# Seven rounds of weight pieces behind the softmaxes, maxima two ahead, and two late stores behind loads, in a graph network with cross-attention

## The chip, the core and the metric

The kernel runs on one core of a Trainium2 chip. The metric is the device time of one launch in microseconds (us). In the profile PE is the matrix engine (TensorE), DVE the vector engine (VectorE), ACT the scalar engine (ScalarE), POOL is GpSimd, and SP (SyncE) issues nearly all DMAs. Each engine works through its own queue in order; an instruction that has to wait holds all that stand behind it on that engine. This holds for SP's queue of DMA issues too.

## The reference

A graph network over 1024 nodes with 512 features: normalise, one graph convolution, four layers of cross-attention and a gated feed-forward network (FFN), one more graph convolution. Cut to its core:

```
def _attn(xf, cond, Wq, Wk, Wv, Wo):          # 16 batches of 64 nodes, 256 condition rows each, 8 heads of 64
    q = (xb @ Wq); k = (cond @ Wk); v = (cond @ Wv)
    att = einsum('bnhd,bmhd->bhnm', q, k) * DH ** (-0.5)
    w = softmax(att, axis=-1)
    o = einsum('bhnm,bmhd->bnhd', w, v)
    return (o @ Wo)

h = _gcn(batchnorm(x))
for i in range(4):
    h = h + _attn(_ln(h), cond, Wq[i], Wk[i], Wv[i], Wo[i])
    u = _ln(h) @ geglu_w[i] + geglu_b[i]       # 512 x 4096
    val, gate = split(u, 2)
    h = h + (val * gelu(gate)) @ ffo_w[i] + ffo_b[i]
h = _gcn(h)
return h + x_in
```

## The kernel before

**Parts.** Matrix products are made from split operands. A matrix is cut into a high part, a low part and a third one (high less low), and three products are summed. So every operand passes through ACT (high part), DVE (low part) and DVE or GpSimd (third part) before PE reads it. For the condition these are `ah_c`, `al_c`, `as_c` (GpSimd's subtraction makes `as_c`, L301); in layer 0 they are made on the way and stored, and in layers 1 to 3 they are loaded as `ch`, `cl`, `cs`.

**Attention.** The 16 batches form eight groups g of two batches (128 nodes). The loop over g = 0 to 5 makes, in each iteration, the keys k of group g+1, its first values v, the mix (`po`, L845) of group g, the scores `sc` of group g+1 (L811), the remaining values, and the output projection (`oy`, `ox`, L883 and L888) of group g, whose operands are `oh` (ACT, L869), `ol` and `os` (DVE, L872 and L873). The last group's softmax stands outside the loop; what is called g=6 below is the work around it, where DVE follows program order. "The softmax of group 5" is traced in iteration g=4.

**Softmax.** `scores` (L800) handles four banks u. For each: DVE takes the maximum `nmax_u` (L818), ACT two exponentials with sums (L823), DVE the reciprocal (L826) and two multiplies (L828) on `pr`. Then PE turns `pr` around (`tr_pr`).

**Weight pieces.** The FFN's up-projection computes a part of its columns from weight blocks that are split into parts ahead of time, during the attention loop. `stage` (L912) splits one 128 x 256 piece: ACT the high part (L917), DVE the low (L918) and third part (L919), then a store into `half_dram` (plain pieces, 8 of them) or `chunk_dram` (14 pieces, of two chunks with seven each, some of them sums and differences made by DVE at L950 to L963). The pieces rotate through two buffers, `gs2`; a piece can only be begun when the store of the piece before the last has landed. `staged` (L922) is a generator that is advanced by eight steps at the end of iterations 3, 4 and 5. Its loads (`gp`, `gx`) are issued in the step that first needs them.

**Order.** PE's order is written out (`pin`). For the other engines a scheduler picks the order from the dependencies and the program order; `in_order`, `issue_after` and `waiting_for` add such dependencies. So a piece of code that is traced elsewhere shifts what stands ahead of what on ACT, DVE and SP.

**Start of the FFN.** Two stages of columns are multiplied first (`g`, L994); DVE writes the gated result `fT` (L1016) and SP stores it to `f_dram` (`Gated.store`, L1233), from which the down-projection reads it much later. Then come chunks: the first two are read from `chunk_dram` (`ga`, `gb`, L1202 and L1214, used at L1109), the others are loaded as raw weights (`gxa`, `gxb`, L1071), summed by GpSimd (L1081) and split by ACT and DVE (`gha`, L1047, L1048). ACT scales PE's results (L1123) and applies the gates (L1138).

Of the kernel before, what the change touches and what calls it, by code (L numbers as in the profile page):

```python
# [9 lines left out]
F32 = mybir.dt.float32  # L10
# [5 lines left out]
OP = mybir.AluOpType  # L16
AX = mybir.AxisListType

P = 128
# [7 lines left out]
def gnn_kernel(  # L27
# [26 lines left out]
    nc = tc.nc  # L54
# [41 lines left out]
    @contextmanager  # L96
    def in_order(engine):

        traced = nc.cur_bb.bb.instructions
        n = len(traced)  # L100
        before = next((i for i in reversed(traced) if i.engine == engine), None)
        yield
        for i in traced[n:]:
            if i.engine == engine:
                if before is not None:
                    tc.add_manual_dep(i, before.name, mybir.DependencyInfo(
                        mybir.DependencyClass.NoSync, mybir.DependencyReason.DATA))
                before = i

    def bank(name):  # L110
        return psum.tile([P, 512], F32, tag="bank", name=name)
# [673 lines left out]
    def acc_tile(name):  # L785
        return accs.tile([P, 512], F32, tag="acc", name=name)
# [13 lines left out]
    def scores(l, g, qT, kT):  # L800


        c0 = (g % 4) * P
        probs = {}
        banks = [bank(f"sc_{l}_{g}_{u}") for u in range(4)]
        for c2 in range(2):
            for a in range(2):
                for j in range(2):
                    pj = slice(j * DH, (j + 1) * DH)
                    for b in range(2):  # L810
                        pin(nc.tensor.matmul(  # L811
                            banks[2 * c2 + j][b * NPG:(b + 1) * NPG, a * M:(a + 1) * M],
                            qT[g // 4][c2][pj, a, c0 + b * NPG:c0 + (b + 1) * NPG],
                            kT[c2][pj, a, b * M:(b + 1) * M], start=True, stop=True))
        for u in range(4):
            ps3 = banks[u].rearrange("p (a m) -> p a m", a=2)
            nmax = small.tile([P, 2], F32, tag="nmax", name=f"nmax_{l}_{g}_{u}")
            nc.vector.tensor_reduce(nmax, ps3, AX.X, OP.max, negate=True)  # L818
            pr = t512(f"pr_{l}_{g}_{u}")
            pr3 = pr.rearrange("p (a m) -> p a m", a=2)  # L820
            tot = small.tile([P, 2], F32, tag="tot", name=f"tot_{l}_{g}_{u}")
            for a in range(2):
                nc.scalar.activation(pr3[:, a, :], ps3[:, a, :], AF.Exp,  # L823
                                     bias=nmax[:, a:a + 1], accum_out=tot[:, a:a + 1])
# [88 lines left out]
    def stage(x, to, name):  # L913

        t = three_halves(f"gs2_{name}")
        h, low, third = (t[:, i * M:(i + 1) * M] for i in range(3))
        nc.scalar.mul(twelve_bits(h), x, INWARD * TINY)  # L917
        nc.vector.scalar_tensor_tensor(twelve_bits(low), h, -1.0 / TINY, x, OP.mult, OP.add)  # L918
        nc.vector.tensor_tensor(twelve_bits(third), h, low, OP.subtract)  # L919
        nc.sync.dma_start(to, t.rearrange("p (w f) -> p w f", w=3))  # L920

    def staged(l):  # L922

        for j in range(2):
            for n in range(2):
                x = acc_tile(f"gp_{l}_{j}_{n}")
                of = geglu_w[l][2 * n * P:2 * (n + 1) * P, j * DFF:j * DFF + PLAIN * P]
                nc.sync.dma_start(x.rearrange("p (k f) -> p k f", k=2),
                                  of.rearrange("(k p) f -> p k f", p=P))
                for k in range(2):  # L930
                    yield
                    stage(x[:, k * M:(k + 1) * M], half_dram[j, 2 * n + k], f"{l}_{j}_{n}_{k}")
        for c in range(PLAIN, KC):
            name = f"{l}_{c}"
            pairs = []
            for k in range(2):
                t = acc_tile(f"gx_{name}_{k}")
                for j in range(2):
                    of = geglu_w[l][2 * k * P:2 * (k + 1) * P, j * DFF + c * P:j * DFF + (c + 1) * P]
                    nc.sync.dma_start(columns_of(t)[:, j], of.rearrange("(k p) f -> p k f", p=P))  # L940
                pairs += [t[:, :M], t[:, M:]]
            a11, a21, a12, a22 = pairs
            s1, s2 = (rows.tile([P, M], F32, tag="gy", name=f"gy{i}_{name}", bufs=2)
                      for i in range(2))

            def put(x, i):
                stage(x, chunk_dram[c - PLAIN, SPLIT.index(i)], f"{name}_{i}")

            yield
            nc.vector.tensor_tensor(s1, a21, a22, OP.add)  # L950
            put(a22, 3)
            yield
            nc.vector.tensor_tensor(s2, s1, a11, OP.subtract)
            put(s1, 4)
            yield
# [4 lines left out]
            yield  # L960
            put(a12, 1)
            yield
            nc.vector.tensor_tensor(a12, a12, s2, OP.subtract)  # L963
            put(s2, 5)
            yield
            put(a12, 2)
            yield

    class HalfWeights:

# [85 lines left out]
    def columns_of(t):  # L1056
        return t.rearrange("p (b k c) -> p b k c", k=2, c=P)

    class Chunk:


        def __init__(self, l, r, c):
            self.n, self.c = f"{l}_{r}_{c}", c
            self.cv = l * 2 * DFF // P + r * KC + c
            self.x = [flat(slot(f"gxa_{self.n}")), t512(f"gxb_{self.n}")]
            self.x.append(rows.tile([P, M], F32, tag="gy", name=f"gy_{self.n}", bufs=2))
            for k, n in enumerate((2, 1)):
                for j in range(2):
                    c0 = j * DFF + r * D + c * P
                    of = geglu_w[l][2 * k * P:2 * (k + 1) * P, c0:c0 + P]  # L1070
                    nc.sync.dma_start(columns_of(self.x[k])[:, n * j],  # L1071
                                      of.rearrange("(k p) f -> p k f", p=P))
            self.parts = [None, None, None]

        def sums(self):
# [385 lines left out]
    for l in range(L):  # L1461
# [166 lines left out]
        for g in range(NG - 2):  # L1628
# [56 lines left out]
        for _ in staging:  # L1685
            pass
        g = NG - 2
        last = l == L - 1
        f_first = Gated(l, 0)
# [398 lines left out]
```

## Time and profile before

| | |
|---|---|
| median of 3 runs | 2278.33 us (2275.65 to 2283.69) |
| profiled execution | 2280.34 us |
| its span in the profile | 2278.4 us |
| granted PE clock | 0.998 of full speed |
| DVE busy | 1722.1 us |
| ACT busy | 1155.4 us |
| GpSimd busy | 507.4 us |

The profile describes one execution. A timeline row gives the start, the duration, the engine, the line and operation, "output <- input", how many like instructions are put together (x4), and in brackets the idle time ahead of it and what ended that. Rows of waits give the engine and its instruction, what it waited for, and then total us, times, longest us. `[0.77 <-DMA ga<-chunk_dram]` reads: idle for 0.77 us, until the load of `ga` from `chunk_dram` had landed. SPq rows are DMA issues, whose duration is that of the issue and not of the transfer.

### The profile page before, as it was taken

What the parts mean: (1) busy time and instruction counts of PE and PEld (TensorE: products, weight loads), DVE (VectorE), ACT (ScalarE), POOL (GpSimd) and SP (SyncE); (2) the same over time, 40 slices, a digit from 0 to 9 for tenths busy, and PEclk for the clock granted to TensorE, in tenths of its full rate; (3) what the DMA queues carried; (4) which work ended last, traced back from release to release, by engine and by line L of the source; (5) the groups of instructions that cost most, each with busy time, mean ns of one, the idle gap of its engine ahead of it and who ended that gap; (6) DMA issues with size and microseconds to landing.
All of it is one profiled execution on the core that took longest, in us unless ns stands there. A gap on an engine that the chain in (4) does not pass through costs nothing. (4 is left out here: it accounts for less than half of the span.)

```text
span 2278.4 us, 35747 instructions
## 1 busy us (share of the span) xinstructions
PE 2241.9 (98%) x12768; PEld 1807.5 (79%) x12768; DVE 1722.1 (76%) x3296; ACT 1155.4 (51%) x2313; POOL 507.4 (22%) x487
## 2 busy tenths in 40 slices
PE   8999999999999999999999999999999999999999
PEld 5678778788888878788888888878888887878787
DVE  9886676999965466899976466889976465789965
ACT  7555546565345445565346445555426445556521
POOL 1121201387000000177000000178100000058301
PEclk9999999999999999999999999999999999999999
DMA  5154554433425264443533364353543355353551
GB/s 171 57 185 167 209 208 140 138 120 130 167 111 194 80 243 172 130 128 102 194 129 142 118 228 174 96 169 102 179 163 135 125 176 197 107 169 111 179 184 54
DMA packets 216952, 340.83 MB, mean 150 GB/s; under 512 B 16488, under 2 KB 117168, under 8 KB 216768
## 3 DMA queue, kind: packets, MB, share of 16 engines
q1 hardware_dynamic: 214672, 333.05, 42.8%
q0 software_dynamic: 1376, 4.30, 0.6%
q8 instruction: 105, 1.72, 0.3%
q10 hardware_dynamic: 720, 1.11, 0.1%
q14 instruction: 79, 0.65, 0.1%
HBM read 236.69 MB, written 101.72 MB: 149 GB/s over the span
## 5 line engine op out<-in xcount | busy, mean ns | idle before, releaser
L1123 ACT ACTIVATE g<-g 128x512 f32<-128x512 f32 x224 | 131.3, 586 | 190.4 <-PE g L1109 187.6
L1581 POOL TENSOR_TENSOR ln3T<-ln3T,ln3T 128x512 f32<-128x512 f32 x8 | 13.3, 1659 | 885.5 <-DVE ln3S L1574 885.5
L1288 PE MATMUL fx<-bs_wff,as_f 128*128 128x512 f32 x512 | 158.8, 390 | 0.0
L1288 PE MATMUL fy<-bl_wff,al_f 128*128 128x512 f32 x512 | 158.6, 390 | 0.0
L1288 PE MATMUL fy<-bh_wff,ah_f 128*128 128x512 f32 x512 | 157.7, 389 | 0.0
L292 ACT ACTIVATE ah_f<-fr 128x1024 fp32r<-128x1024 f32 x64 | 67.9, 1060 | 173.6 <-DVE al_f L293 80.2
L823 ACT ACTIVATE pr<-sc,nmax 128x256 f32<-128x256 f32 x256 | 118.3, 472 | 58.6 <-DVE nmax L818 58.6
L818 DVE TENSOR_REDUCE nmax<-sc 128x2 f32<-128x512 f32 x128 | 84.1, 679 | 77.5 <-PE sc L811 77.5
L361 ACT ACTIVATE k<-k 128x512 f32<-128x512 f32 x125 | 72.8, 585 | 116.5 <-PE k L350 116.5
L361 ACT ACTIVATE v<-v 128x512 f32<-128x512 f32 x127 | 74.5, 587 | 100.5 <-PE v L350 100.4
L1053 POOL TENSOR_TENSOR gsa<-gha,gla 128x512 fp32r<-128x512 f32 x96 | 122.6, 1301 | 6.1 <-DVE gla L1048 6.1
L1109 PE MATMUL g<-gr,gha 128*128 128x512 f32 x384 | 118.2, 389 | 0.0
L1288 PEld LDWEIGHTS fy<-bl_wff,al_f 128*128 128x128 f32 x512 | 96.1, 188 | 21.5 <-DVE bl_wff L1265 1.6
L1288 PEld LDWEIGHTS fx<-bs_wff,as_f 128*128 128x128 f32 x512 | 96.1, 188 | 21.4 <-DVE bs_wff L1269 1.7
L1288 PEld LDWEIGHTS fy<-bh_wff,ah_f 128*128 128x128 f32 x512 | 96.1, 188 | 20.0
L350 PE MATMUL v<-bh_wv,ch 128*128 128x512 f32 x384 | 106.9, 400 | 1.2 <-ACT pr L823 1.2
L293 DVE SCALAR_TENSOR_TENSOR al_f<-ah_f,fr 128x1024 fp32r<-128x1024 f32 x64 | 78.1, 1220 | 35.6 <-ACT ah_f L292 29.5
L350 PE MATMUL k<-ch,bh_wk 128*128 128x512 f32 x384 | 104.0, 392 | 0.0
L350 PE MATMUL v<-bl_wv,cl 128*128 128x512 f32 x384 | 103.1, 390 | 0.0
L350 PE MATMUL v<-bs_wv,cs 128*128 128x512 f32 x384 | 103.0, 391 | 0.0
L350 PE MATMUL k<-cl,bl_wk 128*128 128x512 f32 x384 | 102.8, 389 | 0.0
L350 PE MATMUL k<-cs,bs_wk 128*128 128x512 f32 x384 | 101.6, 395 | 0.6 <-ACT k L361 0.6
(333 smaller groups left out, 5956.8 us busy)
## 6 DMA issues: line engine op xcount, KB each, us to landing
f_dram<-fT SPq DMA_DIRECT2D x128, 256.0 KB, 2.0
fr<-f_dram SPq DMA_DIRECT2D x64, 512.0 KB, 4.6
ch<-cond_dram SPq DMA_DIRECT2D x48, 512.0 KB, 4.9
cl<-cond_dram SPq DMA_DIRECT2D x48, 512.0 KB, 6.5
cs<-cond_dram SPq DMA_DIRECT2D x48, 512.0 KB, 7.8
chunk_dram<-gs SPq DMA_DIRECT2D x56, 384.0 KB, 2.4
wff<-in_L_gnn_ffo_w_dram SPq DMA_DIRECT2D x32, 512.0 KB, 5.4
half_dram<-gs SPq DMA_DIRECT2D x32, 384.0 KB, 3.5
```

What stands on the lines that cost most here:

```text
L292: nc.scalar.mul(twelve_bits(h), x, INWARD * TINY)
L293: left_parts.low = nc.vector.scalar_tensor_tensor(twelve_bits(l), h, -1.0 / TINY, x, OP.mult, OP.add)
L350: pin(nc.tensor.matmul(self.bank, twelve_bits(left[k // 2])[:, k % 2, self.c * P:(self.c + 1) * P], twelve_bits(right[k // 2])[:, k % 2, : ...
L361: nc.scalar.mul(self.bank, self.bank, 1.0 + TINY)
L818: nc.vector.tensor_reduce(nmax, ps3, AX.X, OP.max, negate=True)
L823: nc.scalar.activation(pr3[:, a, :], ps3[:, a, :], AF.Exp, bias=nmax[:, a:a + 1], accum_out=tot[:, a:a + 1])
L1053: split_left.last = pin(t.tensor_tensor(s_at, h_at, l_at, OP.subtract))
L1109: pin(nc.tensor.matmul(to, self.part(i, which)[:, k, :], self.rights[i][which].bitcast(F32R)[:, k, :], start=start and k == 0, stop=stop a ...
L1123: pin(nc.scalar.mul(to, to, 1.0 + TINY))
L1288: pin(nc.tensor.matmul(to, twelve_bits(left[which][0])[:, k, b * P:(b + 1) * P], twelve_bits(right[which])[:, k, :], start=u == 0 and whic ...
L1581: t.tensor_tensor(b12, b22, b12, OP.subtract)
```

## The change

Three edits.

*Softmax.* Two maxima are traced ahead of the loop over u, and each turn of it takes the maximum of u + 2 behind its reciprocal.

*Pieces.* `staged` becomes seven rounds, each of which splits three or four pieces. A round's loads are issued a round ahead (`fetch`), and its instructions are put behind everything that DVE and ACT have been given so far (`behind_traced`). The rounds stand: in the iteration of g=3 in the key loop (i == 1), behind the softmax, and at the end; in that of g=4 in the key loop and behind the softmax; in that of g=5 in the key loop; the first loads are issued in that of g=2. The three places of "eight steps" are gone. The number of pieces is the same.

*Stores.* The second halves of the first two `fT` stores are traced behind the loads of the second raw chunk, and are issued on SP after the last of these.

```diff
+    def behind_traced(*engines):
+        traced = nc.cur_bb.bb.instructions
+        n = len(traced)
+        last = {e: next(i for i in reversed(traced) if i.engine == e) for e in engines}
+        yield
+        for i in traced[n:]:
+            if i.engine in last:
+                tc.add_manual_dep(i, last[i.engine].name, mybir.DependencyInfo(
+                    mybir.DependencyClass.NoSync, mybir.DependencyReason.DATA))
...
+        nmax = {}
+        def largest(u):
+            if u < 4:
+                nmax[u] = small.tile([P, 2], F32, tag="nmax", name=f"nmax_{l}_{g}_{u}")
+                nc.vector.tensor_reduce(nmax[u], banks[u].rearrange("p (a m) -> p a m", a=2),
+                                        AX.X, OP.max, negate=True)
+        largest(0)
+        largest(1)
         for u in range(4):
             ps3 = banks[u].rearrange("p (a m) -> p a m", a=2)
-            nmax = small.tile([P, 2], F32, tag="nmax", name=f"nmax_{l}_{g}_{u}")
-            nc.vector.tensor_reduce(nmax, ps3, AX.X, OP.max, negate=True)
...
             nc.vector.reciprocal(inv, tot)
+            largest(u + 2)
...
     def staged(l):
...
+        def fetch(j):
+            if j < 2:
+                tiles = [acc_tile(f"gp_{l}_{j}_{n}") for n in range(2)]
...
+            else:
+                tiles = [acc_tile(f"gx_{l}_{j}_{k}") for k in range(2)]
...
+        def split(j, pieces):
+            if j < 2:
+                for k, x in enumerate(pieces):
+                    stage(x, half_dram[j, k], f"{l}_{j}_{k}")
+                yield
+                return
...
             nc.vector.tensor_tensor(s1, a21, a22, OP.add)
             put(a22, 3)
-            yield
             nc.vector.tensor_tensor(s2, s1, a11, OP.subtract)
             put(s1, 4)
-            yield
             nc.vector.tensor_tensor(a21, a11, a21, OP.subtract)
             put(a11, 0)
             yield
...
+        for j in range(KC):
+            pieces = fetch(j)
+            yield
+            flow = split(j, pieces)
+            for some in range(1 if j < PLAIN else 2):
+                if some:
+                    yield
+                with behind_traced(mybir.EngineType.DVE, mybir.EngineType.Activation):
+                    next(flow)
...
+                if i == 1 and g > 2:
+                    next(staging, None)
...
             v[1].begin()
             v[0].end()
+            if g in (2, 3, 4):
+                next(staging)
...
-            if g > 2:
-                for _ in islice(staging, 8):
-                    pass
+            if g == 3:
+                next(staging)
...
         load()
-        for c in range(PLAIN):
-            f_first.store(c, (1,))
...
                         sum_chunk(1)
                         load()
+                        with tc.issue_after(ready[-1].loaded.ins):
+                            for n in range(PLAIN):
+                                f_first.store(n, (1,))
```

How this moves instructions, at three places. The first is DVE in layer 0, iteration g=4, around the softmax of group 5 (`nmax_5`); `gs_0_2_5` is piece 5 of layer 0, chunk 2. Before:

```order
L950 TENSOR_TENSOR gy_0_3_17832<-gx_3_0_17826,gx_3_1_17829 128x256
L953 TENSOR_TENSOR gy_0_3_17833<-gy_0_3_17832,gx_3_0_17826 128x256
L293 SCALAR_TENSOR_TENSOR al_c_6_1_0_17344<-ah_c_6_1_0_17343,ct_6_1_17052 128x1024
L918 SCALAR_TENSOR_TENSOR gs_0_3_3_17835<-gs_0_3_3_17835,gx_3_1_17829 128x256
L918 SCALAR_TENSOR_TENSOR gs_0_3_4_17841<-gs_0_3_4_17841,gy_0_3_17832 128x256
L919 TENSOR_TENSOR gs_0_3_3_17835<-gs_0_3_3_17835 128x256
L919 TENSOR_TENSOR gs_0_3_4_17841<-gs_0_3_4_17841 128x256
L956 TENSOR_TENSOR gx_3_0_17826<-gx_3_0_17826 128x256
L818 TENSOR_REDUCE nmax_5_0_17286<-sc_5_0_17266 128x2
L818 TENSOR_REDUCE nmax_5_1_17296<-sc_5_1_17267 128x2
```

and now:

```order
L305 SCALAR_TENSOR_TENSOR al_c_6_0_0_17395<-ah_c_6_0_0_17394,ct_6_0_17105 128x1024
L939 SCALAR_TENSOR_TENSOR gs_0_2_1_17185<-gs_0_2_1_17185,gx_2_1_17048 128x256
L940 TENSOR_TENSOR gs_0_2_1_17185<-gs_0_2_1_17185 128x256
L985 TENSOR_TENSOR gx_2_1_17048<-gx_2_1_17048,gy_0_2_17136 128x256
L305 SCALAR_TENSOR_TENSOR al_c_6_1_0_17402<-ah_c_6_1_0_17401,ct_6_1_17106 128x1024
L939 SCALAR_TENSOR_TENSOR gs_0_2_5_17191<-gs_0_2_5_17191,gy_0_2_17136 128x256
L940 TENSOR_TENSOR gs_0_2_5_17191<-gs_0_2_5_17191 128x256
L832 TENSOR_REDUCE nmax_5_0_17344<-sc_5_0_17324 128x2
L832 TENSOR_REDUCE nmax_5_1_17346<-sc_5_1_17325 128x2
L939 SCALAR_TENSOR_TENSOR gs_0_2_2_17196<-gs_0_2_2_17196,gx_2_1_17048 128x256
```

Behind the second `al_c` stood two whole pieces and one difference ahead of the first maximum; now one piece stands there, and one between the two `al_c`. Line numbers of the new kernel are larger (L918 is now L939, L818 is L832).

The second place is SP's queue at the start of the FFN of layer 0; `fT_0_0` and `fT_0_1` are the gated results, each stored in two halves. Before:

```order
L1233 DMA f_dram<-fT_0_0_18461 128x512
L1233 DMA f_dram<-fT_0_1_18507 128x512
L1233 DMA f_dram<-fT_0_0_18461 128x512
L1071 DMA gxb_1_0_18638<-in_L_gnn_geglu_w_dram 128x2x128 x2
L1202 DMA ga_0_3_0_18582<-chunk_dram 128x4x256
L1202 DMA ga_0_3_1_18583<-chunk_dram 128x4x256
L1202 DMA ga_0_3_2_18584<-chunk_dram 128x4x256
L1071 DMA gxa_1_0_18637<-in_L_gnn_geglu_w_dram 128x2x128 x2
L1233 DMA f_dram<-fT_0_1_18507 128x512
```

and now, with the rows of `gb` between left out:

```order
L1264 DMA f_dram<-fT_0_0_18461 128x512
L1264 DMA f_dram<-fT_0_1_18507 128x512
L1102 DMA gxb_1_0_18638<-in_L_gnn_geglu_w_dram 128x2x128 x2
L1233 DMA ga_0_3_0_18582<-chunk_dram 128x4x256
L1233 DMA ga_0_3_1_18583<-chunk_dram 128x4x256
L1233 DMA ga_0_3_2_18584<-chunk_dram 128x4x256
L1102 DMA gxa_1_0_18637<-in_L_gnn_geglu_w_dram 128x2x128 x2
...
L1102 DMA gxa_1_1_18669<-in_L_gnn_geglu_w_dram 128x2x128 x2
L1102 DMA gxb_1_1_18670<-in_L_gnn_geglu_w_dram 128x2x128 x2
L1264 DMA f_dram<-fT_0_0_18461 128x512
L1264 DMA f_dram<-fT_0_1_18507 128x512
```

The two second halves have moved from ahead of the loads of `gxb`, `ga` and `gxa` to behind those of the next raw chunk.

The third place is ACT in layer 1, iteration g=4; `gs_1_2_2` is piece 2 of chunk 2, `pr_5_0` the first exponentials. Before:

```order
L917 ACTIVATE gs_1_2_2_22720<-gx_2_1_22681 128x256
L368 COPY kT_5_1_22434<-k_5_2_22419 128x512
L861 COPY pT_4_0_22474<-tr_pr_4_0_22469 128x512
L861 COPY pT_4_2_22488<-tr_pr_4_2_22483 128x512
L361 ACTIVATE v_5_0_22502<-v_5_0_22502 128x512
L869 ACTIVATE oh_4_22544<-po_4_22468 128x512
L823 ACTIVATE pr_5_0_22570,tot_5_0_22571<-sc_5_0_22548,nmax_5_0_22568 128x256 x2
```

and now:

```order
L882 COPY pT_4_0_22532<-tr_pr_4_0_22527 128x512
L938 ACTIVATE gs_1_2_1_22455<-gx_2_1_22348 128x256
L882 COPY pT_4_2_22546<-tr_pr_4_2_22541 128x512
L938 ACTIVATE gs_1_2_5_22461<-gy_1_2_22406 128x256
L373 ACTIVATE v_5_0_22560<-v_5_0_22560 128x512
L938 ACTIVATE gs_1_2_2_22466<-gx_2_1_22348 128x256
L890 ACTIVATE oh_4_22602<-po_4_22526 128x512
L843 ACTIVATE pr_5_0_22630,tot_5_0_22631<-sc_5_0_22606,nmax_5_0_22626 128x256 x2
```

Three pieces now stand between the copies of `pT` and the exponentials, where none stood. Their stores share SP's queue with the loads of the condition parts: on SP, `ch_6_0` is now issued between the store of piece 6 and that of piece 1, where all six loads stood behind the store of piece 5 before; the loads of `gx_3_0` (chunk 3) now stand ahead of all six.

More of the change, by code (lines that the diff above doesn't have):

```diff
@@ L823, in scores @@
                 nc.scalar.activation(pr3[:, a, :], ps3[:, a, :], AF.Exp,
-                                     bias=nmax[:, a:a + 1], accum_out=tot[:, a:a + 1])
+                                     bias=nmax[u][:, a:a + 1], accum_out=tot[:, a:a + 1])
             inv = small.tile([P, 2], F32, tag="inv", name=f"inv_{l}_{g}_{u}")
             nc.vector.reciprocal(inv, tot)
+            largest(u + 2)
             for a in range(2):
@@ L922, in staged, with columns @@
     def staged(l):
[L924 to L930, printed above, removed]
-                    yield
[L932 to L942, printed above, removed]
+        def columns(c, n):
+            return geglu_w[l][2 * n * P:2 * (n + 1) * P, c:c + M if c % DFF == 0 else c + P]
+        def fetch(j):
+            if j < 2:
+                tiles = [acc_tile(f"gp_{l}_{j}_{n}") for n in range(2)]
+                for n, t in enumerate(tiles):
+                    nc.sync.dma_start(t.rearrange("p (k f) -> p k f", k=2),
+                                      columns(j * DFF, n).rearrange("(k p) f -> p k f", p=P))
+            else:
+                tiles = [acc_tile(f"gx_{l}_{j}_{k}") for k in range(2)]
+                for k, t in enumerate(tiles):
+                    for i in range(2):
+                        nc.sync.dma_start(columns_of(t)[:, i],
+                                          columns(i * DFF + j * P, k).rearrange("(k p) f -> p k f", p=P))
+            return [of[:, i * M:(i + 1) * M] for of in tiles for i in range(2)]
+        def split(j, pieces):
[4 more added lines that the diff above has]
+                return
+            a11, a21, a12, a22 = pieces
+            name = f"{l}_{j}"
             s1, s2 = (rows.tile([P, M], F32, tag="gy", name=f"gy{i}_{name}", bufs=2)
@@ L1070, in __init__ @@
                     of = geglu_w[l][2 * k * P:2 * (k + 1) * P, c0:c0 + P]
-                    nc.sync.dma_start(columns_of(self.x[k])[:, n * j],
-                                      of.rearrange("(k p) f -> p k f", p=P))
+                    self.loaded = nc.sync.dma_start(columns_of(self.x[k])[:, n * j],
+                                                    of.rearrange("(k p) f -> p k f", p=P))
             self.parts = [None, None, None]
@@ L1678, in gnn_kernel @@
                 turn_cond(g + 3, each=pin)
-            if g > 2:
-                for _ in islice(staging, 8):
-                    pass
+            if g == 3:
+                next(staging)
             if g == NG - 3:
                 add_bias(nc.vector, *range(4))
-        for _ in staging:
-            pass
+        assert next(staging, None) is None
         g = NG - 2
```

8 lines of the change are left out of this document (2 added, 6 removed).

## The prediction

> **What bounds the kernel now.** I read the page first, for whose time this is, and then the waits of TensorE.
>
> ```profile
> span 2278.4 us, 35747 instructions
> ...
> PE 2241.9 (98%) x12768; PEld 1807.5 (79%) x12768; DVE 1722.1 (76%) x3296; ACT 1155.4 (51%) x2313; POOL 507.4 (22%) x487
> ```
>
> PE is busy for 98% and idle for 2278.4 − 2241.9 = 36.5 us. The change gives PE the same instructions in the same order (front part), so it can only move those 36.5 us. The waits of PE by what ended them (total, times, longest), from the rows that the change can reach:
>
> ```profile
> PE v L350 <- ACT v L361: 6.9, 3, 3.9
> PE g L1109 <- ACT g L1123: 4.2, 4, 1.2
> ...
> PE g L1109 <- DMA ga<-chunk_dram: 3.2, 5, 0.8
> PE oy L883 <- DVE ol L872: 1.8, 3, 1.0
> ...
> PE k L350 <- ACT k L361: 1.8, 2, 1.1
> PE v L350 <- ACT pr L823: 1.5, 4, 0.4
> ```
>
> These hold 19.4 us; of the k row only the shorter wait (1.8 − 1.1 = 0.7) is late in the program, the other stands in the start-up. The remaining 17 us of idle time are start-up (edges, pc, begun_k and the like) and the end, where nothing moves.
>
> One correction goes with each wait. PE's timeline of one matmul by itself, and of a stretch without waits:
>
> ```profile
> 309.75 0.39 PE L350 MATMUL k<-as_c,bs_wk 128*128 128x512 f32 x1
> ...
> 408.63 7.42 PE L994 MATMUL g<-gr,gp 128*128 128x512 f32 x32
> ```
>
> One matmul is recorded with 0.39 us, yet 32 take 7.42, so they follow each other every (7.42 − 0.39)/31 = 0.227 us. Idle time is counted from a matmul's recorded end, 0.16 us after its successor would have begun. A wait of w therefore costs w + 0.16.
>
> **The change part by part.**
>
> *A, the late softmaxes of layer 0 (6.6 us of the first row).* Timelines of PE, DVE and GpSimd at g=4, then DVE at g=3, the page's group of the exponentials (instructions, busy us, mean ns), PE and DVE in layer 1, and PE at g=3 of layer 0:
>
> ```profile
> 313.91 1.96 PE L811 MATMUL sc<-kT,qT 64*64 64x256 f32 x32
> ...
> 324.50 1.26 PE L350 MATMUL v<-bs_wv,as_c 128*128 128x512 f32 x4 [3.87 <-ACT v L361]
> ```
> ```profile
> 315.34 0.41 DVE L918 SCALAR_TENSOR_TENSOR gs<-gs,gx 128x256 fp32r<-128x256 f32 x1
> 315.67 1.51 DVE L918 SCALAR_TENSOR_TENSOR gs<-gs,gy 128x256 fp32r<-128x256 f32 x1
> 317.11 1.84 DVE L919 TENSOR_TENSOR gs<-gs 128x256 fp32r<-128x256 f32 x2
> ...
> 319.21 1.28 DVE L818 TENSOR_REDUCE nmax<-sc 128x2 f32<-128x512 f32 x2
> ```
> ```profile
> 315.55 2.78 POOL L301 TENSOR_TENSOR as_c<-ah_c,al_c 128x512 fp32r<-128x512 f32 x2 [1.55 <-PE sc L811]
> ```
> ```profile
> 280.00 1.27 DVE L818 TENSOR_REDUCE nmax<-sc 128x2 f32<-128x512 f32 x2
> ```
> ```profile
> L823 ACT ACTIVATE pr<-sc,nmax 128x256 f32<-128x256 f32 x256 | 118.3, 472 | 58.6 <-DVE nmax L818 58.6
> ```
> ```profile
> 842.11 1.96 PE L811 MATMUL sc<-kT,qT 64*64 64x256 f32 x32
> ```
> ```profile
> 843.24 1.29 DVE L818 TENSOR_REDUCE nmax<-sc 128x2 f32<-128x512 f32 x2 [2.78 <-PE sc L811]
> ```
> ```profile
> 285.30 1.22 PE L350 MATMUL v<-bs_wv,as_c 128*128 128x512 f32 x2 [2.73 <-ACT v L361]
> ```
>
> The piece step L918 takes 0.41 us alone and 1.51 beside GpSimd's as_c subtraction (315.55 to 318.33, two halves of 1.39): it ends when a GpSimd half ends. The maxima come behind these steps. In layer 1, where DVE waits for the scores (842.11 and 843.24), the maximum begins 1.13 us after they do; here it could have begun at 313.91 + 1.13 = 315.04 and began at 319.21, 4.17 late, and PE paid 3.87: the chain has 0.3 us of slack. At g=3 the like: lateness 2.73 + 0.3.
> After the change no piece stands ahead of the first maximum at g=3 (in DVE's order kT, two al_c, then nmax_4_0), so I take the whole 2.73 + 0.16 as saved. At g=4 two pieces remain around the second al_c, 4 steps, of which two or three will be held by a GpSimd half (1.0 to 1.1 each): the maximum at about 317.1 to 318.7, middle 317.9, late by 2.9; less 0.3 of slack, and less 0.9 because ACT now scales the v that PE waits for ahead of the last pair of exponentials (2 × 0.472), leaves 1.7. Saved 3.87 − 1.7 = 2.2. **A = 2.9 + 2.2 = 5.1**; bounds 1 (both places keep most of their pieces' delay) and 6.9.
>
> [...]
>
> *B, the stuck DVE of layers 1 to 3 (oy row).* SP's issues, DVE and PE in layer 1, g=4:
>
> ```profile
> 840.18 0.93 SPq L271 DMA_DIRECT2D cs<-cond_dram  x2
> ...
> 841.64 0.73 SPq L940 DMA_DIRECT2D gx<-in_L_gnn_geglu_w_dram  x1
> ```
> ```profile
> 851.94 0.42 DVE L950 TENSOR_TENSOR gy<-gx,gx 128x256 f32<-128x256 f32 x1 [3.66 <-DMA gx<-in_L_gnn_geglu_w_dram]
> ```
>
> The gx load was issued behind six loads of ch, cl and cs, landed 10.2 us later, and held DVE for 3.66 us ahead of ol, for which PE waited. Now gx_3_0 is issued ahead of all six and gx_3_1 behind two, and its first user stands behind ol. The row goes with its corrections: 1.8 + 3 × 0.16 = **2.3**, and the late k wait, 0.7 + 0.16 = **0.8** likewise (that one I take from its place, behind the same DVE delay in layer 3). Bounds 0 and 3.1.
>
> *C, the softmax of g=6, all layers.* DVE, and PE (the first row is a like group of 8 transposes ahead of it):
>
> ```profile
> 386.36 0.68 DVE L818 TENSOR_REDUCE nmax<-sc 128x2 f32<-128x512 f32 x1
> ...
> 388.87 0.69 DVE L818 TENSOR_REDUCE nmax<-sc 128x2 f32<-128x512 f32 x1
> ```
> ```profile
> 367.64 1.04 PE L205 MATMUL tr_ln<-ident,xn_ln 128*128 128x128 f32 x8
> ...
> 393.17 1.21 PE L350 MATMUL v<-bh_wv,ah_c 128*128 128x512 f32 x4 [0.39 <-ACT pr L823]
> ...
> 396.06 2.17 PE L205 MATMUL tr_pr<-ident,pr 128*128 128x128 f32 x16
> ```
>
> DVE runs in program order here: each maximum follows the multiply of the one before, 2.51 us apart. With the maxima two ahead the exponentials follow each other and the third ends some 3 us earlier. That removes the wait for pr, 1.5 + 4 × 0.16 = 2.1, and what the 16 transposes lose on the last pr, about 0.2 in each layer: 16 in 2.17 us. Eight others in layer 0 took 1.04; with the records' tail of 0.16 or more counted once, 16 would take some 1.9 to 1.95. **C = 2.1 + 0.8 = 2.9**; bounds 2.1 and 2.9.
>
> *D, the third round's loads at the start of the FFN, all layers.* SP, DVE and PE in layer 1:
>
> ```profile
> 953.63 0.32 SPq L1233 DMA_DIRECT2D f_dram<-fT  x1
> ...
> 955.08 1.51 SPq L1202 DMA_DIRECT2D ga<-chunk_dram  x3
> ```
> ```profile
> 949.61 0.68 DVE L1831 SCALAR_TENSOR_TENSOR gl<-ln3S,gr 128x512 fp32r<-128x512 f32 x1
> ...
> 952.86 0.74 DVE L1016 SCALAR_TENSOR_TENSOR fT<-g,gcols,gg 128x512 f32<-128x512 f32 x1
> ```
> ```profile
> 961.29 1.20 PE L1109 MATMUL g<-gr,ga 128*128 128x512 f32 x4 [0.77 <-DMA ga<-chunk_dram]
> ```
>
> SP stood at the store of fT, which waits for DVE's L1016 (ends 953.60); gxb, ga and, next, gxa were queued behind it. The store is now behind them. Then ga's first load needs only DVE's gl step (949.61 + 0.68 = 950.29) and the others PE's and DVE's reads between 950 and 953: 3 to 5 us earlier than 955.08. The longest wait for ga is 0.8. All go: 3.2 + 5 × 0.16 = **4.0**; bounds 2 and 4.0. The store itself is read only by the down-projection, hundreds of instructions later.
>
> *E, the wait behind it.* GpSimd, ACT and PE in layer 1:
>
> ```profile
> 964.54 2.21 POOL L1081 TENSOR_TENSOR gxa<-gxa 128x256 f32<-128x256 f32 x2
> ```
> ```profile
> 966.78 1.06 ACT L1047 ACTIVATE gha<-gxa 128x1024 fp32r<-128x1024 f32 x1 [1.40 <-DMA gxb<-in_L_gnn_geglu_w_dram]
> ```
> ```profile
> 969.56 0.73 PE L1109 MATMUL g<-gs,ga 128*128 128x512 f32 x2 [1.15 <-ACT g L1123]
> ```
>
> GpSimd's sums over the loaded gxa end at 964.54 + 2.21 = 966.75; ACT's gha begins 0.03 later (the row names a load, the sums end last), two gates (L1138) and the scale that PE awaits (L1123) stand behind it, so PE resumes at 969.56. With gxa 3 to 5 us earlier, gha falls into ACT's 1.40 us of idle time and the scale moves forward. I charge 0.3 per layer for what is late next, the gates, which wait for PE's own results: 4.2 + 4 × 0.16 − 4 × 0.3 = **3.6**; bounds 0 (the gates bind) and 4.9.
>
> *New waits, layers 1 to 3, g=4.* ACT's waits, and the page's list of issues (KB each, median us to landing):
>
> ```profile
> ACT gs L917 <- DMA chunk_dram<-gs: 41.8, 24, 5.6
> ```
> ```profile
> chunk_dram<-gs SPq DMA_DIRECT2D x56, 384.0 KB, 2.4
> ```
>
> Piece 2's ACT step now stands directly ahead of oh and the exponentials, and its DVE steps ahead of the maximum (843.24 in the rows under A). It needs one of two piece buffers, free when piece 1's store has landed; that store stands on SP behind one load of ch. DVE's two steps of piece 1 can end at about 839.8; the median store lands 2.4 us after its issue, so 842.2. ACT 842.2 to 842.6, DVE's two steps to 843.45, the maximum 0.2 late, inside the slack of 0.3. Such a wait lasts 41.8/24 = 1.7 us where it occurs. Between nothing and 1.7 + 0.16 in each of three layers, 0 to 5.6 us, I take 0.3 each, **−0.9**, being nearest to the walk.
>
> **Sum.** 5.1 + 2.3 + 0.8 + 2.9 + 4.0 + 3.6 − 0.9 = 17.8. The profiled execution took 2280.34 (its span and 1.9 around it) and becomes 2262.5; the median of the runs is 2.0 lower, 2278.33, and becomes **2260.5**.
>
> **The rivals.**
> 1. *Only FFN and g=6 come.* A and B come back as other waits, because pieces still stand ahead of maxima, and their number is the same. For it: two pieces remain at g=4 of layer 0. Against: g=3 has none left. Gain 2.9 + 4.0 + 3.6 − 0.9 = 9.6: 2268.7.
> 2. *Slower, by the head of ACT's queue.* Piece 2 waits for the landing of a store behind large loads, and exponentials stand behind it. For it: 10.2 us from issue to landing in B. If the store took that in all four layers, it would land at 850.0, 7.8 late, 7.5 past the slack: 4 × (7.5 + 0.16) = 30.6 lost, 17.8 + 0.9 gained: 2290. It makes the kernel slower from a landing that is 18.7/4 + 0.3 = 5.0 us late, 847.2 in layer 1. Against: one large load is ahead, not six.
> 3. *The waits only move.* Seven rounds put three groups of pieces per layer ahead of a softmax; with a wait of 1.7 − 0.3 + 0.16 at each, 12 × 1.56 = 18.7 is lost again: 2278.
> [...]
>
> **How the numbers follow.** Forecast 0.5, rival 4 0.12, rival 1 0.18, rival 3 0.14, rival 2 0.06. What a measurement of this kernel can tell from no change is about 0.3%, 6.8 us. Forecast, rival 4 and nearly all of rival 1 (it loses 0.02 to new waits at their upper bound) are faster: 0.78; rival 3, that 0.02 and a third of rival 2 are the same: 0.18; the rest is slower: 0.04. Range: with every term at its best, 6.9 + 3.1 + 2.9 + 4.0 + 4.9 = 21.8 and no new wait, 2256.5, and the runs scatter by 2.7 below their median: 2254. Upwards to rival 1 with new waits at 5.6: 2268.7 + 4.7, 2274. Left out are rivals 2 and 3.
>
> **What would show it.** PE's waits of after: the rows for ga, ol and pr gone, v for ACT at 2 us in place of 6.9, g for ACT below 1.5. ga issued before 953 in layer 1 and gha without an idle gap. The maximum at g=3 1.1 us behind its scores. I am wrong where ACT's pieces wait ahead of exponentials: PE then shows new rows of v for ACT in layers 1 to 3, and DVE's maxima begin over 1.5 us behind the scores.

## The result: 4.7 us where 17.8 were forecast

The changed kernel takes 2274.49 us (median of 20 runs, 2270.88 to 2281.74), the one before 2279.23 us (20 runs, 2273.61 to 2284.50). The ratio is 0.9981 with a 95% interval of 0.9972 to 0.9990: faster by 2 to 6 us. The prediction was 2260.5 with a range of 2254 to 2274 and is wrong, narrowly by its range and by a factor of nearly four in the gain.

The profiled execution of the changed kernel took 2275.67 us. First the page, for the span and PE's busy time:

```profile
span 2273.9 us, 35755 instructions
...
PE 2240.1 (99%) x12768; PEld 1809.2 (80%) x12768; DVE 1718.2 (76%) x3296; ACT 1156.8 (51%) x2313; POOL 506.6 (22%) x487
```

Then PE's waits (total us, times, longest us), those beyond the start-up:

```profile
PE v L362 <- ACT v L373: 12.6, 6, 3.5
...
PE g L1140 <- DVE g L1160: 2.7, 4, 0.8
...
PE g L1140 <- DVE gl L1864: 0.4, 2, 0.2
```

The rows for `ga`, `ol`, `pr` and `g<-ACT g` are gone, as forecast, and with them the late wait for k. But the row that was to shrink from 6.9 to about 2 us has grown to 12.6. It had three waits and now has six: a small one in the start-up, two in layer 0 (0.67 and 2.75 us), and three new ones, one in each of layers 1 to 3 at g=4. The second row is new: at the start of the FFN, where the waits for `ga` and for ACT's scale have gone, PE now waits for DVE's.

Since PE issues the same 12,768 matmuls in the same order in every kernel of this study, the n-th matmul of two profiles can be laid beside each other. How much its lead or lag changes across a part of the program is what that part gained (−) or lost (+). The table gives this in us against the profile before; the columns on the right are experiments, told below.

| part (all against the kernel before) | forecast | changed kernel | loads behind | piece 2 later | pieces only |
|---|---|---|---|---|---|
| up to g=3 of layer 0 | 0 | +0.1 | +4.3 | +2.2 | +2.8 |
| layer 0, g=3 and g=4 | −5.1 | −5.9 | −7.2 | −3.5 | −5.5 |
| g=6, four layers | −2.9 | −3.7 | −3.7 | −3.7 | 0.0 |
| start of the FFN, four layers | −7.6 | −5.3 | −5.4 | −5.9 | +1.3 |
| layers 1 to 3, g=4 | −2.2 | **+10.2** | −1.9 | −3.1 | +9.9 |

The rest is within 0.3 us. The first row is not put down to the edits: its differences arise at the waits of the start-up (begun_k and the first k), ahead of everything that they move. The last row holds the error.

**Where the new waits come from.** Layer 1, g=4 of the changed kernel: SP's queue, ACT, DVE, PE.

```profile
831.25 0.38 SPq L283 DMA_DIRECT2D ch<-cond_dram  x1
833.28 0.32 SPq L941 DMA_DIRECT2D chunk_dram<-gs  x1
```
```profile
837.54 0.42 ACT L938 ACTIVATE gs<-gx 128x256 fp32r<-128x256 f32 x1 [2.50 <-DMA chunk_dram<-gs]
837.87 0.58 ACT L890 ACTIVATE oh<-po 128x512 fp32r<-128x512 f32 x1
839.51 0.48 ACT L843 ACTIVATE pr<-sc,nmax 128x256 f32<-128x256 f32 x1 [1.06 <-DVE nmax L832]
```
```profile
837.99 0.43 DVE L939 SCALAR_TENSOR_TENSOR gs<-gs,gx 128x256 fp32r<-128x256 f32 x1 [2.51 <-ACT gs L938]
838.45 0.42 DVE L940 TENSOR_TENSOR gs<-gs 128x256 fp32r<-128x256 f32 x1
838.79 1.28 DVE L832 TENSOR_REDUCE nmax<-sc 128x2 f32<-128x512 f32 x2
```
```profile
834.77 1.96 PE L823 MATMUL sc<-kT,qT 64*64 64x256 f32 x32
...
844.10 1.60 PE L362 MATMUL v<-bs_wv,cs 128*128 128x512 f32 x4 [2.61 <-ACT v L373]
845.50 1.91 PE L904 MATMUL oy<-oh,oh 128*128 128x512 f32 x4
```

Read it from SP downwards. Piece 1's store is issued at 833.28, behind a load of `ch`. ACT's step of piece 2 waits for its landing and starts at 837.54, 4.3 us after the issue, where I had used the median of 2.4. DVE waits for ACT, the maximum waits behind DVE's two steps and begins at 838.79 instead of 834.77 + 1.13 = 835.90: 2.9 us late, and PE waits for 2.61, again 0.3 less. In layers 2 and 3 the same stretch, from the issue to ACT's step, takes 5.8 and 6.0 us, and PE waits for 3.5 and 2.75 us.

### The profile page after: what moved, and what is told of

Read it like the earlier page. It is cut to its first block, busy times and chain, and to the rows that moved or that the text cites. A ratio compares the mean times of both kernels' runs of the same rounds, so it can differ in the third digit from the quotient of the medians.

```text
span 2273.9 us, 35755 instructions
## 1 busy us (share of the span) xinstructions
PE 2240.1 (99%) x12768; PEld 1809.2 (80%) x12768; DVE 1718.2 (76%) x3296; ACT 1156.8 (51%) x2313; POOL 506.6 (22%) x487
## 3 DMA queue, kind: packets, MB, share of 16 engines
q8 instruction: 105, 1.72, 0.3%
## 5 line engine op out<-in xcount | busy, mean ns | idle before, releaser
L832 DVE TENSOR_REDUCE nmax<-sc 128x2 f32<-128x512 f32 x128 | 83.6, 678 | 70.6 <-PE sc L823 70.6
```

Source lines behind the costliest of these rows:

```text
L832: nc.vector.tensor_reduce(nmax[u], banks[u].rearrange("p (a m) -> p a m", a=2), AX.X, OP.max, negate=True)
```

## The experiments

The times below are medians beside runs of the kernel before on the same chip; each ratio is to those.

**1. The loads of ch, cl and cs behind piece 2's store.** The pieces stay where they are; in layers 1 to 3 only the loads move.

```diff
-            if l:
+            if l and g != 4:
                 load_parts(l, g + 2)
...
+            if l and g == 4:
+                with tc.issue_after(stage.stored.ins):
+                    load_parts(l, g + 2)
             if g in (2, 3, 4):
                 next(staging)
```

> The changed kernel, except that in layers 1 to 3 the six loads of the condition parts of group 6 (ch, cl, cs) are issued on SP behind the store of piece 2 instead of between the stores of pieces 6, 1 and 5. Theory 1 (landing): PE's new waits in layers 1 to 3 (three of the v<-ACT v row, 8.9 us) come from piece 2 waiting for the landing of piece 1's store behind a load of ch, so the three waits fall to under 0.5 us each, and the time falls by 8 to 9.5 us against the changed kernel, to about 0.994 of before. Theory 2 (work): it is the amount of piece work ahead of the maxima on DVE and ACT, whatever the loads do: the three waits stay above 2 us each and the time does not change. A possible price under both: the loads of cs land some 2 us later, which may show as waits of PE's k for DMA.

2265.62 us, ratio 0.9938 (0.9924 to 0.9951), some 9 us under the changed kernel. SP, ACT, and PE at the same place (later by 4 us in this execution, from the start-up):

```profile
835.82 0.34 SPq L941 DMA_DIRECT2D chunk_dram<-gs  x1
```
```profile
838.39 0.42 ACT L938 ACTIVATE gs<-gx 128x256 fp32r<-128x256 f32 x1 [1.33 <-DMA chunk_dram<-gs]
```
```profile
844.94 1.19 PE L362 MATMUL v<-bs_wv,cs 128*128 128x512 f32 x4 [0.59 <-ACT v L373]
845.97 1.10 PE L904 MATMUL oy<-oh,oh 128*128 128x512 f32 x4
```

From issue to ACT's start it is now 2.6 us instead of 4.3. The three waits are 0.59, under 0.2 and 0.23 us (expected: under 0.5 each, so the first is a little above). With the same pieces in the same places, theory 2 is out. No wait for `cs` appeared. The other profiles agree. In the changed kernel and in experiments 2, 4 and 6 to 8, where `ch` loads stand on SP around piece 1's store in layers 1 to 3, it landed 4.2 to 5.9 us after its issue in all 18 places (4.2, 5.7 and 5.9 in the changed kernel). Where the loads are moved away (experiments 1, 3 and 5), it took 2.3 to 3.4 us in eight of nine; the ninth is told under experiment 5. Whether the load ahead of the store or the one right behind it does this, no run separates.

**2. Piece 2 one round later.** The loads stay between the stores; only piece 2 moves behind the softmax.

```diff
             put(s2, 5)
-            put(a12, 2)
             yield
+            put(a12, 2)
...
+                    if not some:
+                        for last in late:
+                            next(last, None)
```

> The changed kernel, except that piece 2 of each chunk is split one round later, behind the next softmax (the loads of ch keep their place between the stores). If piece 2's wait for a piece buffer is what holds ACT and DVE ahead of the maxima in layers 1 to 3 (theory 1 of the run with the condition loads behind), the three waits fall to under 0.7 us each here too, though piece 1's store still lands late, and the time is 8 to 10 us under that of the changed kernel (about 0.994 of before). If the late loads themselves mattered (theory 3: the ch transfers disturb something else, such as the v operands), the waits stay. A price may be that DVE now waits for gx_3_1, which can only be loaded after piece 2, behind ol: up to 3 us of DVE time, which I expect to cost PE nothing.

2265.23 us, ratio 0.9938 (0.9920 to 0.9956). No wait of v for ACT is left in layers 1 to 3. So the late store does no harm once nothing ahead of a maximum needs its buffer. In layer 0 the wait at g=4 became longer (4.04 us in place of 2.75), which I had not expected. By the profile the first maximum comes 0.3 us later than in the changed kernel, and ACT scales the v that PE waits for behind all eight exponentials, where two of them (0.47 us each) came after it before.

**3. Both.** The loads behind piece 5's store and piece 2 one round later, from the two diffs above.

> Both single cures together: the condition loads of group 6 issued behind piece 5's store, and piece 2 split one round later. If both act on the one wait of piece 2 for its buffer, they do not add: the three waits of layers 1 to 3 are gone as with either alone, layer 0 is as with the later piece alone (about 4 us at g=4), and the time is the same as either within 2 us, 2263 to 2267. The loads of cl and cs now stand behind gx_3_1, which waits for piece 2: if they land after PE's k needs them, waits of k for DMA cs of 1 to 4 us per layer appear and the time is 3 to 10 us longer than with either alone.

2269.5 us, ratio 0.9951 (0.9935 to 0.9966). Not better, but 3 us (by the ratios) to 4 us (by the medians) worse than either; the intervals of the ratios still overlap. SP's queue and PE's waits:

```profile
840.90 1.67 SPq L283 DMA_DIRECT2D ch<-cond_dram  x2
848.22 0.90 SPq L958 DMA_DIRECT2D gx<-in_L_gnn_geglu_w_dram  x2
849.21 0.89 SPq L283 DMA_DIRECT2D cl<-cond_dram  x2
```
```profile
PE k L362 <- DMA cl<-cond_dram: 2.7, 4, 1.1
```

The `gx` loads wait for piece 2 to be read, SP stands still from 842.6 to 848.2, and `cl` (I had named `cs`) comes too late for k. The same error as in the change itself, one queue further: a wait on SP, here of 5.6 us, held the loads behind it.

**4. GpSimd behind the softmax, layer 0.** What is left in layer 0 comes in the main from DVE's steps being held by GpSimd; at g=3 of the changed kernel DVE and GpSimd show it without any piece (272.90 is the same operation alone: 1.21 us, against 2.24 beside `as_c`):

```profile
272.90 1.21 DVE L305 SCALAR_TENSOR_TENSOR al_c<-ah_c,ct 128x1024 fp32r<-128x1024 f32 x1
275.70 2.24 DVE L305 SCALAR_TENSOR_TENSOR al_c<-ah_c,ct 128x1024 fp32r<-128x1024 f32 x1 [1.58 <-POOL as_c L313]
277.86 1.27 DVE L832 TENSOR_REDUCE nmax<-sc 128x2 f32<-128x512 f32 x2
```
```profile
274.34 2.52 POOL L313 TENSOR_TENSOR as_c<-ah_c,al_c 128x512 fp32r<-128x512 f32 x2 [27.43 <-PE v L362]
```

```diff
-                split_cond(g + 2, None if g else scores.last)
+                with waiting_for(scores.last, mybir.EngineType.Pool) if g > 1 else nullcontext():
+                    split_cond(g + 2, None if g else scores.last)
```

> The changed kernel, except that in layer 0, from iteration g=2 on, GpSimd's subtractions as_c wait for the last multiply of the softmax. Theory 1 (lock): what is left of the waits of layer 0 at g=3 and g=4 (0.67 and 2.75 us) comes from DVE steps with two SBUF inputs being held while GpSimd subtracts; with GpSimd out of the way they run in 0.42 (pieces) and 1.22 us (al_c), the maxima of g=4 begin about 3 us earlier, and both waits fall to under 0.5 us: 2.5 to 3.7 us less than the changed kernel. Theory 2 (count): the pieces ahead of the maxima cost that time by their number, and at least 1.5 us remain. Layers 1 to 3 are unchanged by it, 8.9 us under both.

2276.90 us, ratio 0.9991 (0.9978 to 1.0003): no gain. The two waits did fall, from 0.67 and 2.75 us to none and 0.39, and the steps ahead of the maxima at g=4 run in 0.42 and 1.22 us, as expected of steps that nothing holds. The fall at g=4 is not the hold's alone, though: the order on DVE changed with it, and the second `al_c` and L985 now stand behind the first maxima. And GpSimd's third parts are now late: at g=4 the first begins at 322.22, 10.1 us behind the scores, where in the changed kernel it begins 0.7 us ahead of them. New waits for the condition's loads and for `hall` (0.8 us) take the place of the old ones:

```profile
PE v L362 <- ACT v L373: 7.9, 5, 3.7
...
PE tr_cond L217 <- DMA cond<-in_L_gnn_cond_dram: 2.4, 2, 2.1
```

The 7.9 us of v are the three waits of layers 1 to 3 (2.10, 3.67 and 1.52) with 0.39 of layer 0 and the start-up's.

**5. Loads behind, and GpSimd behind the second maximum.** Experiment 1, and in layer 0 an earlier release.

```diff
+                with waiting_for(scores.top[1], mybir.EngineType.Pool) if g > 1 else nullcontext():
+                    split_cond(g + 2, None if g else scores.last)
```

> Condition loads of group 6 behind piece 2's store (as in the run that did this alone), and in layer 0, from iteration g=2 on, GpSimd's subtractions as_c wait for the second maximum of the softmax, not for its last multiply. If DVE steps held by GpSimd are what is left at g=3 and g=4 of layer 0, those two waits (0.66 and 2.77 us there) fall to under 0.5 us together, and, as_c being done some 5 us earlier than with the wait for the last multiply, the new waits for the condition loads (2.1 us) and for hall (0.8) do not come: 2 to 3.5 us under the run with the loads alone, about 2262. If the pieces' number is what counts at g=4, more than 1.5 us stay there.

2276.16 us, ratio 0.9985 (0.9972 to 0.9998), 10.5 us worse than experiment 1. A miss, in three ways, as far as this profile goes; it is of the slowest of the twelve executions, 7.9 us above their median, so not all of what follows need be in the others. The condition's loads wait already at g=2 (PE idle for 2.47 us at 264.93). At g=4 the scheduler now puts piece 5's ACT step between the first maximum and the exponentials, where it waits 2.17 us for a store, and PE waits for 3.6. And DVE's multiplies fall beside GpSimd (the one here takes 1.37 us, where one alone takes 0.35): DVE, then GpSimd:

```profile
326.39 1.37 DVE L850 TENSOR_SCALAR pr<-pr,inv 128x256 f32<-128x256 f32 x1
327.68 0.41 DVE L941 TENSOR_TENSOR gs<-gs 128x256 fp32r<-128x256 f32 x1
```
```profile
324.89 2.72 POOL L313 TENSOR_TENSOR as_c<-ah_c,al_c 128x512 fp32r<-128x512 f32 x2 [29.47 <-ACT gs L939]
```

In layer 1, where this kernel has the SP order of experiment 1, the store that took 2.6 us there let ACT go only 4.8 us after its issue in this profile (848.85 to 853.69), with no load of `ch` ahead, and PE waited for 3.9. The trace hints at what held it: a single packet of 16 KB on the DMA queue for instructions (q8) began at 849.84, while the store's data moved, and took 1.99 us (the median of such packets in this trace is 1.02), and from 853 to 854 the DMA engines were busy for 0.06 of their time, as much as one engine of 16. That this packet put one engine behind is likely, but no run tests it. In these runs the loads were enough for a late landing (4.2 to 5.9 us), but not its only cause (4.8 without them), and PE's chain, with 0.3 us of slack, waited behind each.

**6 and 7. The softmax edit undone; the store edit undone.**

```diff
-        largest(0)
-        largest(1)
         for u in range(4):
+            largest(u)
...
-            largest(u + 2)
```

> The changed kernel with its softmax edit undone (each maximum taken in its own turn). Theory 1: the edit is worth what the waits of before at g=6 were, so four waits of v for pr of 0.4 us return and each group of 16 transposes takes 0.2 us longer, 2 to 3 us in all. Theory 2: the other edits already give DVE the room, and nothing returns at g=6. At g=4 of layers 1 to 3 both expect the 8.9 us to stay within 0.5 us, since the scheduler had taken maxima early there already.

2279.72 us, ratio 0.9996 (0.9987 to 1.0005). By the matching of matmuls each of the four stretches at g=6 loses the 0.94 us that the changed kernel gained there, 3.7 us in all (2 to 3 expected); the new waits of layers 1 to 3 stay (8.8 us).

```diff
-                        with tc.issue_after(ready[-1].loaded.ins):
-                            for n in range(PLAIN):
-                                f_first.store(n, (1,))
...
+        for c in range(PLAIN):
+            f_first.store(c, (1,))
```

> The changed kernel with its store edit undone (the second halves of the first two stores of fT ahead of the loads again). Theory 1: the loads of ga, gxa and gxb fall back by 3 to 5 us, the rows g<-DMA ga (3.2) and g<-ACT g (4.2) return, the row g<-DVE g L1160 (2.7) goes, and the kernel is 4 to 5.5 us slower than the changed one. Theory 2: the loads are held by something else (buffers read late), the rows of after stay and the time is the same within 1 us.

2281.71 us, ratio 1.0013 (1.0004 to 1.0023). The waits are back, and the new row for DVE is gone:

```profile
PE g L1140 <- DMA ga<-chunk_dram: 3.9, 4, 1.8
...
PE g L1140 <- ACT g L1154: 3.2, 3, 1.2
```

The start of the FFN is 6.5 us slower than in the changed kernel (+1.2 against −5.3), above the 4 to 5.5 expected; 1.6 us of it are eight matmuls at half clock behind a wait of 1.78 us for `ga` in layer 0 (last section).

**8. The pieces edit alone**, with the softmax and the stores as before (both diffs above on the changed kernel).

> The kernel before with the pieces edit alone (softmax and stores as before). By the steps between equal matmuls of the two traces, the pieces edit took 5.9 us off layer 0, 3.1 us off the waits for ol and k, and put 13.2 us on layers 1 to 3 (waits of 9.4 and some 3.9 us at half clock behind them): so 2 to 6 us slower than before, ratio 1.001 to 1.0025, with the waits of g=6 and of the FFN as before. If the edits depend on each other, the time comes out outside that.

2287.0 us, ratio 1.0032 (1.0019 to 1.0045). By itself the largest edit of the three makes the kernel slower, by 7.3 us at the median, somewhat more than expected; the part that I had left out is +1.3 us at the start of the FFN, where its later loads and stores meet the stores of `fT` (PE waits for `ga` for 4.1 us in six waits, against 3.2 in five before). The waits of g=6 (1.6 us, against 1.5) and of the FFN for ACT (4.3, against 4.2) are as before.

## Why the prediction was wrong, point by point

- **What bounds the kernel** was right: PE's order is fixed, and all differences are waits and what follows them. What it left out: PE's busy time is not fixed by its instructions. It lies between 2237.5 and 2245.5 us in the ten profiles (2241.9 before, 2240.1 in the changed kernel), with the same matmuls, because some of them run at half clock behind long waits (four in 1.91 us, against 1.10 at full clock). So the change could move more than the 36.5 us of idle time, and a wait of w cost w + 0.16 only where it was short (last section).
- **A, layer 0**: 5.1 forecast, 5.9 measured. At g=3 not all went: 0.67 us stayed, because I counted only pieces as held by GpSimd and not `al_c`, which took 2.24 us beside it, against 1.21 alone. At g=4 the maximum came 4.0 us after it could have, not 2.9, since three steps (two of pieces and the difference L985: 1.41, 1.40 and 1.49 us) were held for 1.0 us each, so 2.75 us of wait stayed in place of 1.7. The gain came out higher all the same, because a long wait cost more than w + 0.16, and the kernel before had two of them here (2.73 and 3.87 us), with 13 and 8 matmuls at half clock behind them, 4.2 us that the forecast did not count. Two errors of opposite sign: that A came out near is luck.
- **B, the stuck DVE**: 3.1 forecast. The gain is there in full, and visible where nothing covers it: −3.1 in the column "piece 2 later". (0.7 + 0.16 is nearer to 0.9 than to the 0.8 written.)
- **C, g=6**: 2.9 forecast, 3.7 measured. Wait and transposes were right in kind; each layer gave 0.94 us in place of 0.73.
- **D and E, the FFN**: 7.6 forecast, 5.3 measured. Both rows went, but what is late next was not the 0.3 per layer that I charged: DVE's scaling (`L1160`, 2.7 us in four waits, 3.3 with 0.16 for each, against the 1.2 charged).
- **New waits, layers 1 to 3**: 0.9 forecast, about 13.3 measured (+10.2, and the 3.1 of B that they cover). **This is the step that failed.** The mechanism was in the text, with its place, its slack of 0.3 us and even the sentence that the store stands behind one load of ch. Its size was off, in three ways. First, I put a store of the median duration, 2.4 us, into a queue whose state was not the median: from its issue to ACT's step it took 4.3, 5.8 and 6.0 us in layers 1 to 3. Second, in layer 1 the store was issued 1.5 us ahead of the scores (833.28 against 834.77), where the walk had it 2.3 ahead (839.8 against 842.11); of the 2.7 us by which the maximum came later than forecast, some 1.9 are the store's duration and 0.8 its issue. Third, w + 0.16 put nothing for the matmuls at half clock behind such waits, 3.8 us. I had also bounded each wait by the mean of ACT's existing waits for stores, 1.7 us, where the same row gave 5.6 as the longest; the three took 2.6, 3.5 and 2.75. The sign named for being wrong is what came: new rows of v for ACT in layers 1 to 3, and the maximum 4.0 us behind its scores in layer 1.
- **The rivals**: rival 2, the head of ACT's queue, is what happened, with 2.6 to 3.5 us per layer in place of the 7.5 at which I had priced it; it had a chance of 0.06 as one that mostly ends slower than before, and no case of mine covered its sizes between 5.6 us in all and that. (Its sums were off too: the loads of ch stand in three layers, not four, and the landing from which it is slower is 18.7/4 − 0.16 + 0.3 = 4.8 us late, not 5.0.) Rival 1 is out, since A and B came. Rival 3 is nearest in time, with 2278, but not in kind: PE waits at one group of pieces in each of layers 1 to 3 and at two in layer 0, not at all twelve. Rival 4, at 0.12, was that GpSimd's subtractions hold the multiplies of the softmax too. No row of before shows that, since none of its 256 multiplies fell beside a subtraction, so it was open. It came, but was small here: at g=3 of the changed kernel one multiply ran into a subtraction and lost 0.12 us (0.47 against 0.35), the larger hold fell on `al_c`, and experiment 5 shows the full size, 1.37 us against 0.35 (last section).
- **The range** ended at 2274, which rested on new waits of 5.6 us at most.

The other terms, by the table, came to 18.0 us (5.9, 3.1, 3.7 and 5.3) where 18.7 were forecast, but only because A and C came out above and D and E below. No one kernel here shows the sum: with the new waits of layers 1 to 3 all but removed it takes 2265.2 to 2265.6 us, 13.3 to 14.5 under before and some 5 above the forecast of 2260.5. That is experiment 1 or 2, each a change of few lines, and faster than both kernels.

## What to carry to other kernels

Where a change puts a step that needs a recycled buffer ahead of the step that the critical engine waits for, the buffer's release is part of the critical path: look at what stands ahead of the releasing transfer in its queue, and price it with the transfers of that queue at that place (here 4.3 to 6.0 us from issue to use), not with a median (here 2.4). If the slack is a few tenths of a microsecond (here 0.3), treat every such wait as exposed. Price a rival over its whole range, not only at its worst: here a small version of an unlikely disaster is what came.

## What the hardware showed that was not expected

**Most long waits of PE were paid for twice.** Behind the 2.61 us wait of the changed kernel above, four matmuls take 1.91 us (845.50), in experiment 1 behind 0.59 us they take 1.10 (845.97). The granted clock of these stretches, changed kernel and then experiment 1 (columns: window, its length, PE busy and matmuls, PEclk, DMA share, GB/s):

```profile
843.00:848.50 5.50, 4.40 (x12) 0.69 0.95 382
848.50:854.00 5.50, 5.50 (x25) 1.00 0.46 181
```
```profile
844.00:849.50 5.50, 4.91 (x22) 1.00 1.00 380
```

Matmuls that follow each other at 0.227 us elsewhere did so at 0.427 for a while here: 12 begin in 4.40 us of PE's time, against 22 in 4.91. Over all ten profiles, past the first 100 us and ahead of matmuls of 512 columns: behind 73 waits of 0.50 to 1.76 us no such stretch, behind eight of 13 waits of 1.78 to 2.84 us, and behind all 14 waits of 3.1 us and more. It lasted 6 to 13 matmuls and cost 1.2 to 2.6 us. The 13.3 us of layers 1 to 3 are, to 0.1, 8.9 us of waits, 0.5 us of the correction, and 3.8 us of slow matmuls behind two of the three.

Between 1.78 and 2.84 us the traces part by where the wait fell. In the profiles of before and of the changed kernel the stretches of half clock begin a whole number of 3.413 us apart (12 and 584 of them behind the first before; 154, 307 and 573 in the changed kernel), and last 3.413 or 6.827 us, but for the last one of each, at the program's end. Cut into steps on that grid, from 100 us on and without the last 20, the two profiles have five steps at full clock in which PE was idle for 1.95 and 2.44 us (before) and for 2.75, 2.61 and 2.16 us (changed kernel). In the step behind each of them the clock was halved. In no other step at full clock was PE idle for more than 1.72 us, and behind none of those was it halved. Layers 1 and 3 of the changed kernel show both cases; the rows are steps of the grid:

```profile
841.27:844.68 3.41, 0.80 (x4) 1.00 0.86 294
844.68:848.09 3.41, 3.41 (x10) 0.50 0.90 367
```
```profile
1889.17:1892.58 3.41, 1.69 (x8) 1.00 0.84 275
1892.58:1895.99 3.41, 2.38 (x10) 1.00 1.01 394
```

The 2.61 us of layer 1 fall into one step, and the next runs at half clock. The 2.75 us of layer 3 fall across two, with 1.72 and 1.03 us, and no slow matmul follows. The grid lies differently in the two profiles (a step begins 1.21 us after the start of the span before, 1.59 in the changed kernel), so whether such a wait was paid for twice was luck here.

**GpSimd also held a multiply with one tensor input.** In experiment 5 sixteen multiplies of `pr` overlap GpSimd's subtractions, and fifteen are held: they take 0.42 to 1.47 us, where one alone takes 0.35, and each ends 0.15 us after a half of the subtraction (the row at 326.39 above is one). The sixteenth began 0.2 us ahead of GpSimd and took 0.35. At g=3 of layer 0 one multiply is held for 0.9 us in experiment 3, and one for 0.1 us in the changed kernel (two multiplies in 0.73 us instead of 0.61), beside a subtraction from 279.32 to 280.61:

```profile
280.30 0.73 DVE L849 TENSOR_SCALAR pr<-pr,inv 128x256 f32<-128x256 f32 x2
```
